# Softmax normalised before the transpose, and the attention output laid out by transfers, in a two-layer image kernel

## The chip, the cores and the metric

The kernel runs on one core of a Trainium2 chip. The metric is the time of one execution on the device in microseconds (us); lower is better. The time before is the median of three runs.

## The reference, cut to what matters

The input is 8 images of 384 channels, 64 x 64 pixels, in float32. Two layers follow, each a residual over a group norm.

Layer 0 is windowed attention. A layer norm over the channels, then queries, keys and values for 8 heads of 48 channels. Heads 0 to 3 ("branch 0") work in windows of 8 x 8 pixels, heads 4 to 7 ("branch 1") in the same windows on an image rolled by 4 pixels both ways, with a mask. Then a projection.

Layer 1 mixes channels, multiplies 8 x 8 patches in the frequency domain by a filter, applies a 3 x 3 convolution to each channel alone ("taps"), gates one half with the GELU of the other, and projects back.

```python
attn = jnp.einsum('bhnd,bhmd->bhnm', q, k) + bias (+ mask)
attn = jax.nn.softmax(attn, axis=-1)
out = jnp.einsum('bhnm,bhmd->bhnd', attn, v)
...
x = x + layer0(group_norm(x))      # out @ proj_w + proj_b
x = x + layer1(group_norm(x))      # w_in, patch filter, 3x3 taps, gelu gate, w_out
```

## The kernel before, in words

**Tiling.** An image is cut into 8 strips of 8 rows (512 pixels). A strip is a tile of 128 partitions by 3 x 512 values: channels on partitions, three groups. Each strip has 8 windows of 64 pixels. A *unit* is one branch of one strip; there are 8 x 8 x 2 = 128 of them.

**Attention of a unit.** `qk_tile` makes queries and keys (`pq`, three PSUM tiles; ScalarE moves them out, L420). `v_tile` makes the values with pixels on partitions (`pvv`, L454), and puts a column of ones beside each head's 48 channels, so that the product with the weights also gives their sum. `scores` makes the scores (`pS`): 32 matmuls of 64 x 64, four of them in the four quadrants of the array at a time. `weights`, on VectorE, adds the position bias (L482), takes each row's maximum (L486) and subtracts it (L489). `exponent` is one ScalarE instruction over 128 x 1024 (L495). `turn` transposes the exponentials on TensorE, 8 transposes `pT` (L72), and ScalarE copies them to `eT` (L505). `apply` multiplies them with the values: 32 matmuls of 64 x 49, `pA`, pixels on partitions. `normalise`, on VectorE, divides by the sums (L529, L530) into `o`. `put` turns `o` to channels on partitions, again by 8 TensorE transposes (`po`), and ScalarE and VectorE copy these into the strips' tiles `oT` (L553, L554, L561 to L563). Branch 1 goes to two strips, since its image is rolled. `project` multiplies `oT` by the projection (`pr`) and VectorE adds it to the input (`x_add`, L572).

**Layer norm.** The sums over channels are matmuls (`ln`); ScalarE copies them (L362), VectorE and ScalarE make the reciprocal deviation `lr` (L364 to L367). It is spread over all partitions by two transfers from SyncE's queue (SP): `lr` to a line in memory (L374), and the line to every partition as `rs` (L376). VectorE multiplies the strip by it: `y<-rs` (L389). Before that, the normalised input `y` comes from VectorE (L338) and its square `sq` from ScalarE (L347).

**Layer 1.** `mix` (`pt`), `transform` (`pf`, L627), `back` (`pz`) and `border` (ScalarE copies of `z`, L655 to L659); the taps on VectorE (L693 for the first on ScalarE, then L699, eight in turn for each of three channel groups); `gate`; `finish` (`pw`, with a PSUM tile of its own `pw2`, then L738 and L740). In the last image, some taps are matmuls with diagonal matrices (`conv_taps`, `pc`): five of group 1 in every strip, and in the last strip nine of group 1 and three of group 2.

**What orders the work.** Every piece of work is entered in a plan with a place, `at(place, piece, ...)`, and the plan is sorted. A unit takes one step of place, a strip two. Layer 1 of an image runs beside layer 0 of the next: strip by strip the two are interleaved. Matmuls keep the plan's order. The other engines' orders are made by the scheduler of the tile framework, with a few fixed dependences. Tiles come from pools with a set number of buffers, handed out in turn: whoever takes a buffer waits until the last reader of its former content is done. In PSUM there are four buffers "gemm" of one bank and two buffers "att" of two banks; `pS`, `pT`, `pA`, `po`, `pw2` and `pc` share the two. A common strip takes the "att" buffers in the order pA, pS, pw2, po, pT, pA, pS, po, pT.

**Empty instructions.** TensorE's instructions are counted as they are built (`FETCHES`, `WAITS`, `RUN_AT`), and empty ones are put among the long matmuls[...].

Of the kernel before, what the change touches and what calls it, by code (L numbers as in the profile page):

```python
# [27 lines left out]
C_SWAP = C_PICK + 2  # L28
N_CONST = C_SWAP + 128
WAITS = 5.325, -22  # L30
FETCHES = {"qk_tile": 12, "v_tile": 24, "project": 12, "scores": 128, "apply": 128, "turn": 16, "put": 16,
# [7 lines left out]
def block_kernel(ctx: ExitStack, tc: tile.TileContext, out, x, consts, fsel, wqk, wv, bqk, bv,  # L39
# [52 lines left out]
    swap = cst[:, C_SWAP:C_SWAP + P]  # L92
# [259 lines left out]
    def ln_sums(b, s):  # L352


        p = psum(f"ln_{b}_{s}")
        for to, t, n in ((0, ys[b, s], KC), (P, ys.pop((b, s, "sq")), 1 if summed(b, s) else KC)):
            for k in range(n):
                for j in range(4):
                    matmul(p[32 * j:32 * (j + 1), to:to + P], ones_c[:, 0:32], t[:, k, j * P:(j + 1) * P],
                           start=(k == 0), stop=(k == n - 1))  # L360
        m = sb.tile([P, 2 * P], F32, tag="lc", bufs=1, name=f"m_{b}_{s}")
        nc.scalar.copy(m, p[:, 0:2 * P])  # L362
        rc = sb.tile([P, P], F32, tag="lr", bufs=2, name=f"lr_{b}_{s}")
        nc.vector.tensor_tensor(rc, m[:, 0:P], m[:, 0:P], ALU.mult)  # L364
        nc.vector.tensor_tensor(rc, m[:, P:2 * P], rc, ALU.subtract)
        nc.scalar.activation(rc, rc, AF.Sqrt, bias=eps_t)
        nc.vector.reciprocal(rc, rc)  # L367
        if (b, s) == (0, 0):
            ys[b, s, "rc"] = rc
            return  # L370

        line = dr.tile([4, P], F32, tag="line", bufs=4, name=f"line_{b}_{s}")
        queue = nc.scalar if b == 0 and s < 2 else nc.sync
        queue.dma_start(out=line, in_=rc[0:P:32, :])  # L374
        rs = ys[b, s, "rs"] = row512("rs", 2, f"rs_{b}_{s}")
        queue.dma_start(out=rs, in_=bass.AP(line.tensor, line.offset, [[0, P], [1, ST]]))  # L376
# [63 lines left out]
    def v_tile(b, s, br, g):  # L440

        y = y2s[b, s] if br else ys[b, s]
        if g == 0:
            v = sb.tile([P, 4, 4, HD + 1], F32, tag="v", bufs=2, name=f"v_{b}_{s}_{br}")
            nc.gpsimd.memset(v[:, :, :, HD:HD + 1], 1.0)
            vs[b, s, br] = v
        v = vs[b, s, br]
        pvv = psum(f"pvv_{b}_{s}_{br}_{g}")
        for i in range(2):
            pair = 2 * g + i  # L450
            for k in range(KC):
                matmul(pvv[:, i * 192:(i + 1) * 192], y[:, k, pair * P:(pair + 1) * P],
                                 wv_sb[:, k, br * 192:(br + 1) * 192], start=(k == 0), stop=(k == KC - 1))
        nc.scalar.copy(v[:, 2 * g:2 * g + 2, :, 0:HD],  # L454
                       pvv[:, 0:384].rearrange("p (g h d) -> p g h d", g=2, h=4))
# [37 lines left out]
    def exponent(b, s, br):  # L493
        e = qks[b, s, br, "e"]
        nc.scalar.activation(e, e, AF.Exp)  # L495

# [11 lines left out]
    def apply(b, s, br):  # L508

        eT, v = qks.pop((b, s, br, "eT")), vs.pop((b, s, br))  # L510
        pA = psum2(f"pA_{b}_{s}_{br}")
        for i in range(2):
            for h in range(4):
                to = (i * 4 + h) * (HD + 1)
                for odd in range(2):
                    pair = 2 * i + odd
                    for q in range(2):
                        rows, half = slice(q * 64, (q + 1) * 64), (q + odd) % 2
                        col = pair * P + (h + q) % 2 * 64
                        matmul(pA[half * 64:(half + 1) * 64, odd, to:to + HD + 1],  # L520
                               eT[rows, h // 2, col:col + 64], v[rows, pair, h, :], start=True, stop=True)
        qks[b, s, br, "A"] = pA

    def normalise(b, s, br):
        nm = f"{b}_{s}_{br}"
        o = os_[b, s, br] = sb.tile([P, 2, 2, 192], F32, tag="o", bufs=1, name=f"o_{nm}")
        pA = qks.pop((b, s, br, "A"))[:, :, 0:8 * (HD + 1)].rearrange("p g (h d) -> p g h d", h=8)
        rc = small.tile([P, 2, 8], F32, tag="rc", bufs=2, name=f"rc_{nm}")
        nc.vector.reciprocal(rc.unsqueeze(3), pA[:, :, :, HD:HD + 1])  # L529
        nc.vector.tensor_tensor(  # L530
            o.rearrange("p g i (h d) -> p g (i h) d", d=HD),
            pA[:, :, :, 0:HD], rc.unsqueeze(3).to_broadcast([P, 2, 8, HD]), ALU.mult)
# [7 lines left out]
    def put(b, s, br):  # L540


        o = os_.pop((b, s, br))
        p = psum2(f"po_{b}_{s}_{br}")
        po = []
        for a in range(2):
            for pair in range(4):
                transpose(p[:, a, pair * P:(pair + 1) * P], o[:, pair % 2, pair // 2, a * 64:a * 64 + P],
                          swap if pair % 2 else ident)
            po.append(p[:, a].rearrange("p (w r c) -> p r w c", w=NS, r=WS))  # L550
        if br == 0:
            oT = out_tile(b, s)
            nc.scalar.copy(oT[:, 0].rearrange("p r (w c) -> p r w c", c=WS), po[0])  # L553
            nc.vector.tensor_copy(oT[64:P, 1].rearrange("p r (w c) -> p r w c", c=WS), po[1][64:P])  # L554
            return
        for half, oT in ((0, out_tile(b, s)), (1, out_tile(b, (s + 1) % NS))):
            to, of = slice(4 - 4 * half, 8 - 4 * half), slice(4 * half, 4 * half + 4)
            for rows, kt, src, copy in ((slice(0, 64), 1, po[0], nc.vector.tensor_copy),
                                        (slice(0, P), 2, po[1], nc.scalar.copy)):
                d = oT[rows, kt, to]  # L560
                copy(d[:, :, 4:60].rearrange("p r (w c) -> p r w c", c=WS), src[rows, of, 0:7])  # L561
                copy(d[:, :, 60:64], src[rows, of, 7, 0:4])
                copy(d[:, :, 0:4], src[rows, of, 7, 4:8])  # L563
# [101 lines left out]
    on_pe = {s: {1: 5} for s in range(NS)}  # L665
    on_pe[NS - 1] = {1: 9, 2: 3}

    def tap_matrices():
        d = strip("y", 3, "taps").rearrange("p k (t c) -> p (k t) c", c=P)
        for m, n, to in ((1, 9, 0), (2, 3, 9)):  # L670
            for i in range(n):
                nc.scalar.activation(d[:, to + i], ident, AF.Copy, scale=dw_sb[:, m, TAPS[i]:TAPS[i] + 1])
        zs["taps"] = {1: d[:, 0:9], 2: d[:, 9:12]}

    def conv_taps(b, s):
        pc = psum2(f"pc_{b}_{s}")
        for i, (m, n) in enumerate(on_pe[s].items()):
# [6 lines left out]
    def conv(b, s, m, tap):  # L684

        z = zs[b, s, m]
        n = on_pe[s].get(m, 0) if b == B - 1 else 0
# [59 lines left out]
    for b in range(B):  # L747
# [22 lines left out]
        for s in range(NS):  # L770
# [16 lines left out]
            for br in range(2):  # L787
# [10 lines left out]
                at(w + 1.07, normalise, b, s, br)  # L798
                at(w + 1.23, put, b, s, br)
# [12 lines left out]
        at(first + 1.90, second_std, b)  # L812
        if b == B - 1:
            at(first + 2, tap_matrices)
        for s in range(NS):
# [16 lines left out]
            if b == B - 1:  # L832
# [11 lines left out]
    for i, (piece, args) in enumerate(order):  # L844
        count += 4 * sum(on_pe[args[1]].values()) if piece is conv_taps else FETCHES.get(piece.__name__, 0)
# [19 lines left out]
def _constants():  # L865
# [6 lines left out]
    c[:, C_SWAP:C_SWAP + P] = np.roll(np.eye(P), 64, axis=1)  # L872
# [96 lines left out]
```

## Time and profile before

| what | value |
|---|---|
| time, median of 3 runs (lowest to highest) | 3695.2 us (3693.99 to 3695.85) |
| time of the profiled execution | 3693.57 us |
| its span, first to last instruction | 3691.7 us |
| mean clock granted to TensorE | 0.994 |
| transposes `po` (L72), 1024 | 133.0 us of records, overlapped |
| normalising, L529 and L530, 128 each | 29.8 and 122.5 us on VectorE |
| exp, L495, 128 | 135.3 us on ScalarE |
| share of the 16 transfer engines taken by SP's queue q1 | 28.4% |

The span is the time that the profile covers; 1.9 us of the profiled execution lie around it. The profile gives for each engine how long it was busy, and for each group of instructions the mean duration of one and the idle time of its engine just before, with the engine that ended it. Matmuls overlap, so their records add up to more than the time that passes; how long a run of matmuls takes is read from the start of one run to the start of the next in the timeline. "DVE" is VectorE, "ACT" ScalarE, "PE" TensorE, "POOL" GpSimd and "SP" SyncE.

### The profile page before, as it was taken

Reading aid. Unit: us, or ns where it says so; the run is one execution under the profiler, and the core shown is the slowest. Engines: PE = TensorE matmul, PEld = TensorE weight load, DVE = VectorE, ACT = ScalarE, POOL = GpSimd, SP = SyncE. Lnnn points to the kernel's source line nnn. Section 1 sums busy time; section 2 is a strip of 40 time slices with the busy share of each in tenths; the row PEclk is TensorE's granted clock in tenths of the full one; section 3 lists DMA queues with packets and bytes.
Section 4 is the critical chain, followed back from the end, with each engine's and each line's share of the span. In section 5 each row is a group of like instructions: output and inputs, shape, how many; then the busy total and the mean of one; then the engine's idle time right before and its main releaser. Section 6 shows DMA issues by size and latency. Waiting matters only on the chain.

```text
span 3691.7 us, 92911 instructions
## 1 busy us (share of the span) xinstructions
PE 3610.3 (98%) x38584; PEld 2342.0 (63%) x38584; DVE 2841.1 (77%) x4607; ACT 2384.6 (65%) x3946; POOL 426.9 (12%) x764
## 2 busy tenths in 40 slices
PE   6999999999999999999999999999999999999898
PEld 4666666666666666666666666666666666666554
DVE  5655578778878788877888778878788777777898
ACT  3776577667667576666766666666676666776442
POOL 4111111101111111111111111111111111110000
PEclk8999999999999999999999999999999999999999
DMA  4222223223323233223333223323233222222422
GB/s 121 87 101 82 77 93 126 84 90 127 118 92 108 79 120 132 96 83 117 118 107 107 104 90 118 119 81 118 98 110 119 92 90 93 93 81 84 152 103 78
DMA packets 144355, 377.07 MB, mean 102 GB/s; under 512 B 12288, under 2 KB 12876, under 8 KB 143948
## 3 DMA queue, kind: packets, MB, share of 16 engines
q1 hardware_dynamic: 139952, 370.60, 28.4%
q8 instruction: 319, 5.23, 0.6%
q0 software_dynamic: 2048, 0.15, 0.1%
q14 instruction: 88, 0.72, 0.1%
q10 hardware_dynamic: 1948, 0.37, 0.1%
HBM read 270.28 MB, written 100.79 MB: 101 GB/s over the span
## 4 chain that ended last, share of the span: by engine, by line
PE 87%; DVE 6%; DMA 3%; ACT 2%; issue 1%; SPq 0%; ACTq 0%; DVEq 0%
PE pq L62 25%; PE pr L62 13%; PE pvv L62 12%; PE pt L62 12%; PE pw L62 6%; DVE zz L699 3%; PE pS L62 3%; PE pA L62 3%; PE po L72 3%; PE pT L72 3%; PE pz L62 3%; PE pf L62 2%; PE ln L62 2%; DMA x_norm<-in_x_dram 1%; DMA x1d<-x_add 0%
## 5 line engine op out<-in xcount | busy, mean ns | idle before, releaser
L699 DVE SCALAR_TENSOR_TENSOR zz<-z,dw_sb,zz 128x512 f32<-128x512 f32 x1490 | 1082.0, 751 | 23.7 <-ACT z L658 11.2
L62 PE MATMUL pq<-y,wqk_sb 128*128 128x512 f32 x2160 | 990.1, 596 | 0.0
L62 PEld LDWEIGHTS pq<-y,wqk_sb 128*128 128x128 f32 x2160 | 402.3, 190 | 436.6 <-issue 403.7
L62 PE MATMUL pt<-wi_sb,xn 128*128 128x384 f32 x1536 | 534.6, 486 | 0.0
L62 PE MATMUL pr<-oT,wp_sb 128*128 128x512 f32 x1152 | 523.1, 592 | 0.5 <-DVE oT L563 0.5
L62 PE MATMUL pvv<-wv_sb,y 128*128 128x192 f32 x2880 | 495.8, 326 | 0.0
L62 PEld LDWEIGHTS pvv<-wv_sb,y 128*128 128x128 f32 x2880 | 471.7, 190 | 36.2 <-issue 23.2
L420 ACT ACTIVATE qab<-pq,bq_sb,cst 96x512 f32<-96x512 f32 (+1 forms) x256 | 198.0, 773 | 383.4 <-PE pq L62 381.5
L62 PEld LDWEIGHTS pt<-wi_sb,xn 128*128 128x128 f32 x1536 | 286.1, 190 | 200.9 <-issue 38.5
L420 ACT ACTIVATE kcd<-pq,vec 32x512 f32<-32x512 f32 x512 | 348.8, 681 | 9.1
L62 PEld LDWEIGHTS pr<-oT,wp_sb 128*128 128x128 f32 x1152 | 211.1, 190 | 223.9 <-issue 213.5
L402 POOL COPY y<-y 128x384 f32<-128x384 f32 x112 | 100.2, 895 | 1528.5 <-PE pvv L62 1021.3
L610 ACT COPY t<-pt 128x384 f32<-128x384 f32 x256 | 124.2, 485 | 176.9 <-PE pt L62 172.9
L364 DVE TENSOR_TENSOR lr<-m 128x128 f32<-128x128 f32 x64 | 18.7, 292 | 281.0 <-ACT m L362 281.0
L693 ACT ACTIVATE zz<-z,dw_sb 128x512 f32<-128x512 f32 x183 | 133.9, 733 | 156.2 <-PE pw L62 141.8
L350 POOL TENSOR_TENSOR sq<-sq 128x512 f32<-128x512 f32 x122 | 156.6, 1284 | 628.1 <-ACT sq L347 623.3
L420 ACT ACTIVATE qcd<-pq,bq_sb,cst 96x512 f32<-96x512 f32 (+1 forms) x256 | 197.4, 771 | 44.7 <-PE pq L62 41.2
L454 ACT COPY v<-pvv 128x384 f32<-128x384 f32 x256 | 121.0, 478 | 156.7 <-PE pvv L62 156.5
L572 DVE SCALAR_TENSOR_TENSOR x_add<-pr,vec,x_add 128x512 f32<-128x512 f32 x192 | 143.5, 747 | 93.6 <-PE pr L62 91.7
L62 PE MATMUL pw<-zz,wo_sb 128*128 128x512 f32 (+1 forms) x512 | 182.3, 499 | 0.0
L420 ACT ACTIVATE kab<-pq,vec 96x512 f32<-96x512 f32 (+1 forms) x256 | 174.3, 681 | 8.3 <-PE pq L62 6.5
L72 PEld LDWEIGHTS pT<-cst,e 128*128 128x128 f32 x1024 | 119.0, 141 | 66.6 <-issue 39.6
(142 smaller groups left out, 5294.9 us busy)
## 6 DMA issues: line engine op xcount, KB each, us to landing
x_add<-in_x_dram SPq DMA_DIRECT2D x64, 768.0 KB, 9.8
x1d<-x_add SPq DMA_DIRECT2D x64, 768.0 KB, 3.7
x_mix<-x1d SPq DMA_DIRECT2D x64, 768.0 KB, 4.4
x_finish<-x1d SPq DMA_DIRECT2D x64, 768.0 KB, 6.0
out_dram<-x_finish SPq DMA_DIRECT2D x64, 768.0 KB, 3.8
x_norm<-in_x_dram SPq DMA_DIRECT2D x61, 768.0 KB, 7.5
x_stats<-in_x_dram SPq DMA_DIRECT2D x56, 768.0 KB, 7.9
rs<-line SPq DMA_DIRECT2D x62, 256.0 KB, 3.0
```

The lines of the kernel that those rows point to most:

```text
L62: tc.keep_in_program_order(nc.tensor.matmul(*args, **kw))
L72: tc.keep_in_program_order(nc.tensor.transpose(*args, **kw))
L350: nc.gpsimd.tensor_tensor(sq[:, 0, :], sq[:, 0, :], sq[:, k, :], ALU.add)
L364: nc.vector.tensor_tensor(rc, m[:, 0:P], m[:, 0:P], ALU.mult)
L402: nc.gpsimd.tensor_copy(dst[:, :, :, :, 0:4], src[:, :, :, :, 4:8])
L420: return nc.scalar.activation(dst[to:to + n], pq[of:of + n], AF.Identity, bias=bias[of:of + n], scale=scale)
L454: nc.scalar.copy(v[:, 2 * g:2 * g + 2, :, 0:HD], pvv[:, 0:384].rearrange("p (g h d) -> p g h d", g=2, h=4))
L572: nc.vector.scalar_tensor_tensor(t[:, m, :], pr, bp_sb[:, m:m + 1], t[:, m, :], ALU.add, ALU.add)
L610: nc.scalar.copy(t1, pt[:, 0:C])
L693: nc.scalar.activation(zz.rearrange("p (r c) -> p r c", c=SW), z[:, 1:9, 1:SW + 1], AF.Copy, scale=dw_sb[:, m, 4:5])
L699: i = nc.vector.scalar_tensor_tensor(acc.rearrange("p (r c) -> p r c", c=SW), z[:, dy:dy + 8, dx:dx + SW], dw_sb[:, m, TAPS[tap]:TAPS[tap] ...
```

## The change

The row sums are no longer made with the values. After exp, VectorE sums each row of 64, takes the reciprocal and multiplies the row by it; the transposed weights are then already normalised. The column of ones and `normalise` go. (`v` keeps 16 zero columns behind its 768, which the last head's 64-column block reaches into.)

`apply` swaps its operands: the values stand in the array, 64 columns of them for a head of 48 channels, and the weights stream through. So `pA` has channels on partitions, and `put` needs no transposes. ScalarE copies `pA` to `o`, pixels in image order (two copies for branch 0, four for branch 1), and transfers on SP's queue bring `o` to the partitions of `oT`: 5 for branch 0, twice 5 for branch 1, of 16 to 48 partitions each.

The tile `o` is larger, and `lr` has one buffer for two. The matrix `swap` goes. `put` stands at `w + 1.07`, where `normalise` was. The last strip of image 6 gets five taps of group 1 as matmuls, the last strip of image 7 five of group 2 for three; the matrices take two tiles. The second group norm's deviation of the last image is entered at 1.995 instead of 1.90. The constants of the empty instructions are set anew.

```diff
-WAITS = 5.325, -22
-FETCHES = {..., "put": 16, ...}
+WAITS = 6.63, -32
+FETCHES = {...}
...
-        rc = sb.tile([P, P], F32, tag="lr", bufs=2, name=f"lr_{b}_{s}")
+        rc = sb.tile([P, P], F32, tag="lr", bufs=1, name=f"lr_{b}_{s}")
...
-            v = sb.tile([P, 4, 4, HD + 1], F32, tag="v", bufs=2, name=f"v_{b}_{s}_{br}")
-            nc.gpsimd.memset(v[:, :, :, HD:HD + 1], 1.0)
+            v = sb.tile([P, 16 * HD + 16], F32, tag="v", bufs=2, name=f"v_{b}_{s}_{br}")
+            nc.gpsimd.memset(v[:, 16 * HD:], 0.0)
...
     def exponent(b, s, br):
         e = qks[b, s, br, "e"]
         nc.scalar.activation(e, e, AF.Exp)
+        rc = small.tile([P, 2 * NS], F32, tag="rc", bufs=2, name=f"rc_{b}_{s}_{br}")
+        nc.vector.tensor_reduce(rc, e, AX.X, ALU.add)
+        nc.vector.reciprocal(rc, rc)
+        nc.vector.tensor_tensor(e, e, rc.unsqueeze(2).to_broadcast([P, 2 * NS, 64]), ALU.mult)
...
     def apply(b, s, br):
         eT, v = qks.pop((b, s, br, "eT")), vs.pop((b, s, br))
         pA = psum2(f"pA_{b}_{s}_{br}")
-        for i in range(2):
-            for h in range(4):
-                to = (i * 4 + h) * (HD + 1)
...
-                        matmul(pA[half * 64:(half + 1) * 64, odd, to:to + HD + 1],
-                               eT[rows, h // 2, col:col + 64], v[rows, pair, h, :], start=True, stop=True)
+        for hp in range(2):
+            for pair in range(4):
+                to = (hp * 4 + pair) * 64
+                for par, q in ((0, 0), (1, 1), (0, 1), (1, 0)):
+                    rows, of = slice(q * 64, (q + 1) * 64), (pair * 4 + hp * 2 + par) * HD
+                    col = pair * P + (par + q) % 2 * 64
+                    matmul(pA[par * 64:(par + 1) * 64, q, to:to + 64], v[rows, of:of + 64],
+                           eT[rows, hp, col:col + 64], start=True, stop=True)
...
-    def normalise(b, s, br):
...
     def put(b, s, br):
-        o = os_.pop((b, s, br))
-        p = psum2(f"po_{b}_{s}_{br}")
-        po = []
-        for a in range(2):
-            for pair in range(4):
-                transpose(p[:, a, pair * P:(pair + 1) * P], o[:, pair % 2, pair // 2, a * 64:a * 64 + P],
-                          swap if pair % 2 else ident)
...
+        pA = qks.pop((b, s, br, "A")).rearrange("p o (h w r c) -> p o h w r c", h=2, w=4, r=WS)
+        o = sb.tile([P, 2, ST], F32, tag="o", bufs=1, name=f"o_{b}_{s}_{br}")
+
+        def columns(first, n, step=16, c=WS):
+
+            return bass.AP(o.tensor, o.offset + first, [list(o.ap[0]), [ST, 2], [step, n], [SW, WS], [1, c]])
+
         if br == 0:
...
+            for q in range(2):
+                nc.scalar.copy(columns(q * WS, 4), pA[:, q])
+            parts = ((slice(0, WS), 0, out_tile(b, s)),)
+        else:
+            nc.scalar.copy(columns(4, 4), pA[:, 0])
+            nc.scalar.copy(columns(12, 3), pA[:, 1, :, 0:3])
+            nc.scalar.copy(columns(60, 1, c=4), pA[:, 1, :, 3:4, :, 0:4])
+            nc.scalar.copy(columns(0, 1, c=4), pA[:, 1, :, 3:4, :, 4:8])
+            parts = ((slice(4, 8), 0, out_tile(b, s)), (slice(0, 4), 256, out_tile(b, (s + 1) % NS)))
+        edge = (P, 64)[br]
+        for rows, of, oT in parts:
+            n = (rows.stop - rows.start) * SW
+            for h in range(4):
+                row = h % 2 * 64 - h * HD
+                for a, z in ((h * HD, min((h + 1) * HD, edge)), (max(h * HD, edge), (h + 1) * HD)):
+                    if a < z:
+                        to = a + br * P + (64 if a >= edge else 0)
+                        nc.sync.dma_start(out=oT[to % P:to % P + z - a, to // P, rows],
+                                          in_=o[row + a:row + z, h // 2, of:of + n])
...
-    on_pe = {s: {1: 5} for s in range(NS)}
-    on_pe[NS - 1] = {1: 9, 2: 3}
+    on_pe = {(B - 1, s): {1: 5} for s in range(NS - 1)}
+    on_pe[B - 2, NS - 1] = {1: 5}
+    on_pe[B - 1, NS - 1] = {2: 5, 1: 9}
...
-                at(w + 1.07, normalise, b, s, br)
-                at(w + 1.23, put, b, s, br)
+                at(w + 1.07, put, b, s, br)
...
-        at(first + 1.90, second_std, b)
+        at(first + (1.90 if b < B - 1 else 1.995), second_std, b)
```

## The prediction

> **What bounds the kernel now.** I read the page first, busy shares and then the chain that ended last, and after these the timelines of single strips of images 4 and 6.
>
> ```profile
> PE 3610.3 (98%) x38584; PEld 2342.0 (63%) x38584; DVE 2841.1 (77%) x4607; ACT 2384.6 (65%) x3946; POOL 426.9 (12%) x764
> PE 87%; DVE 6%; DMA 3%; ACT 2%; issue 1%; SPq 0%; ACTq 0%; DVEq 0%
> ```
>
> TensorE is busy all the time and 87% of the chain is its matmuls. In the steady state it does not stop at all: the stretches from 1852.8 to 1907.5 and from 1907.5 to 1962.2 us, one strip each, show 54.70 us of PE in 54.70 us. So each microsecond that TensorE need not work is won, and each that it must wait is lost.
>
> What decides is how near the softmax comes to the transposes `pT` that need it. Times below count from the end of a unit's `pS` (its last score). Strip 4 of image 4, branch 1, has `pS` end at 1937.1:
>
> ```profile
> 1935.93 0.95 DVE L367 RECIPROCAL lr<-lr 128x128 f32<-128x128 f32 x1 [0.17 <-ACT lr L366]
> 1937.03 0.96 DVE L530 TENSOR_TENSOR o<-pA,rc 128x768 f32<-128x768 f32 x1
> 1938.83 0.68 DVE L482 TENSOR_TENSOR e<-pS,bias 128x512 f32<-128x512 f32 x1
> 1940.20 1.22 DVE L486 TENSOR_REDUCE mx<-e 128x16 f32<-128x1024 f32 x1
> 1941.60 1.76 DVE L389 TENSOR_TENSOR y<-y,rs 128x1536 f32<-128x1536 f32 x1 [0.18 <-DMA rs<-line]
> 1943.28 1.22 DVE L489 TENSOR_TENSOR e<-e,mx 128x1024 f32<-128x1024 f32 x1
> ```
>
> ```profile
> 1945.87 1.06 ACT L495 ACTIVATE e<-e 128x1024 f32<-128x1024 f32 x1
> ```
>
> ```profile
> 1950.85 1.04 PE L72 MATMUL pT<-cst,e 128*128 128x128 f32 x8
> ```
>
> exp ends at +9.8 and `pT` starts at +13.8, so 3.9 us are free. `y<-rs` (layer norm of a later strip) sits in the middle of the chain and starts when its transfer lands, at +4.5. In the first two strips of an image less TensorE work lies between, and nothing is free; this is strip 1 of image 6 (`pS` end 2665.2), where TensorE already waits 1.10 us for exp:
>
> ```profile
> 2668.71 5.32 PE L62 MATMUL pq<-y,wqk_sb 128*128 128x512 f32 x12
> 2675.13 1.09 PE L72 MATMUL pT<-cst,e 128*128 128x128 f32 x8 [1.10 <-ACT e L495]
> ```
>
> The third view is the one wait of TensorE on L530:
>
> ```profile
> 2636.34 0.66 PE L62 MATMUL pw<-g,wo_sb 64*64 64x256 f32 x8 [0.87 <-DVE o L530]
> ```
>
> `pw2` of `finish` takes the PSUM buffer that `pA` held (two buffers "att", taken in turn: pA, pS, pw2). Once L530 was late, and TensorE stood. Normally L530 ends at +0.4, and `pw2` is due at about +0.8 (the first eight `pw` records take 0.7 us from +0.0).
>
> [...]VectorE idles 0.18 us at `y<-rs` with the softmax's next step queued behind. [...]The trace has 3.0 us for `rs<-line` (256 KB) from issue to landing.
>
> **The change, part by part.** Durations are from the page's groups and these timelines; back to back an instruction costs about 0.1 us less than its mean. Orders are those of the instruction lists of the two built kernels.
>
> *Removed on TensorE:* the 8 transposes `po` of a unit. From 1914.02 to 1914.89 they take 0.88 us; 128 units give 112.6 us at most, kept only where TensorE sets the pace.
>
> *Widened:* `pA` goes from 49 to 64 columns, again 32 matmuls. `pS`, with 64, takes 0.95 us against 0.88: 128 x 0.05 = 6 us.
>
> *VectorE:* L529, L530 and the copies L554, L561-L563 go (29.8 + 122.5 + 44.5 + 48.4 + 40.1 = 285 us). Row sums, reciprocal and product over 128x1024 come. They are priced as L486 (1.22), L529 (0.27) and L489 (1.24): 2.7 us x 128 = 349 us. VectorE is not full (45.7 of 54.7 us), so the 64 us more are free as busy time. But these three stand between exp and `pT`, and the built order puts other work among them. Branch 1 of a common strip reads: three adds, `y<-rs`, maximum, subtract, tap, residual, tap, statistics, SUM, tap, reciprocal, tap, PRODUCT. `y<-rs` stands ahead of the maximum now. The walk: the adds start at +0.7 (L530 is gone) and end at +2.0; `y<-rs` waits for its transfer, +4.5, or +4.9 with two of the new transfers ahead of it on SP's queue[...] (bounds +4.5 and +6.2); it ends at 6.5, maximum 7.7, subtract 8.9, exp 10.0. VectorE meanwhile does tap 0.66, residual 0.67, tap 0.66, statistics 0.61 to 11.5, SUM 12.7, tap, reciprocal, tap 14.3, PRODUCT 15.55. `pT` starts at +15.6; TensorE was ready at 13.8 - 0.88 = 12.9, and `pr`, `pvv` and `pz` stand behind it. Against before, `pT` comes 1.8 us later, the saved `po` already counted. By kind of branch-1 unit:
> - 34 common ones: 34 x 1.8 = 61 us.
> - Strip 5 of images 1 to 6, where `y<-rs` comes even ahead of the adds: +16.5 for +13.8, 6 x 2.7 = 16.
> - Strip 0 of images 2 to 7 (four taps and three tiny steps in the gap): +16.1 for +8.9, 6 x 7.2 = 43.
> - Strip 1 of images 2 to 7 (four taps): +15.6 for +9.7, 6 x 5.9 = 35.
> - Image 0, strips 0 and 1 of image 1 and the last two units, walked alike: +9.
>
> Sum 164 us. Branch 0 of images 1 to 7 has 8.3 us free and needs 5.5 to 6 more; there `po` is won: 56 x 0.88 = -49.
>
> *Release of `pA`, an added wait:* now ScalarE frees it, by two or four copies into `o` (0.5, 0.4, 0.1, 0.1 = 1.1 us back to back). Queued ahead on ScalarE are the second `v` copy (ready at -3.8 before the next `pS` end), the square of `y` (1.48), then nine copies and scalings of `z` (6.45 to 9.53 in 1906.45 to 1909.53: 3.1 us). From -3.3 that gives -1.8, +1.3, and with `o` +2.4. `pw2` was due at +0.8, so TensorE waits 1.55 us, and all of `pw`, `pq` behind it. Where statistics of the next image precede the last `y` on VectorE (strips 2 and 3, 11 times), the square is late by 1.2 more: 2.75. Finishes in the dense part: 52; 41 x 1.55 + 11 x 2.75 = 94 us. Bounds: 0, if ScalarE comes early, and 140.
>
> *Transfers:* 5 + 10 per strip, 960 in all, on SP. Issues there last 0.3 to 0.6 us for like ones, so ten need 3 to 6 us of a queue that mostly waits (L741 alone 1112 us). `pr` reads `oT` about a unit later (20 us): nothing. For the last image's end, `oT` comes by transfer: about +4 with the taps. *Taps:* five more on TensorE for strip 7 of image 6 (5 x 0.86), two more at the end, against four and two VectorE steps of 0.66 us in a stretch where VectorE is as full as TensorE (223 and 225 of 251 us): put at nothing, bounds -4 and +6. *Layout:* one buffer for `lr` waits only for a transfer done a strip ago: nothing.
>
> Sum: 164 - 49 + 94 + 6 + 4 = +219. The profiled execution took 3693.6 us (span 3691.7); with it 3912.6. The median of the runs is 1.6 above it: **3914 us**.
>
> **Rivals.**
> - *ScalarE frees `pA` in time* (its queue runs ahead while TensorE waits at `pT`): 3914 - 94 = 3820. Against it: the square cannot start before `v` and the last `y`.
> - *SP delays `rs`*: two issues ahead of it of 1.2 us, as `x_stats` shows at 1916.83, make `rs` 1.3 us later in 52 units: 3914 + 68 = 3982. For it: SP waits for `o` between `line` and `rs`; against it: the `line` transfer takes that time anyway.
> - *The other side, faster:* the three steps fit into the free 3.9 us. They are 2.7 us long, L529 and L530 (1.16 us) go ahead of the chain, and the table load (1.28) no longer waits for the subtract. If `pT` of branch 1 is ready at +12.9, all of `po` is won: 3695.2 - 112.6 + 6 + 4 = 3593. Against it: `rs` lands at +4.5 whatever VectorE does, and strips 0 and 1 have nothing free at all.
> - That `po` might not be gone is excluded: the built list has none.
>
> **Numbers.** Chances: main case 0.65 (its own range 3840 to 3985, from the bounds of `rs` and half the `pw2` wait), free `pA` 0.14, late `rs` 0.12, faster 0.07, and 0.02 that losses and gains cancel within 0.2% (what a measurement can tell from no change). The range goes from 3780, under the first rival, to 4000; it leaves out the faster case and the ends. Faster by over 0.2% 0.07, within 0.2% 0.02, slower 0.91.
>
> **What would show it.** Right: `pT` with waits on VectorE's product of 2.5 to 3 us in common branch-1 units and 6 to 8 in strips 0 and 1, summing to some 220 us (they count from the shortened work, and so are larger than the delays above); `pw` with waits of 1 to 3 us on ScalarE's copies of `o`; a common strip of 57 to 58.5 us for 54.7; PE near 90% (3510 of 3912 us). Wrong: `pT` of branch 1 at +13 or earlier, `y<-rs` with idle time far from 2.5 to 3 us, or new waits of `pr` for `oT`.

## The result, and the profile after

The changed kernel takes 4025.0 us (median of 4 runs, 4024.0 to 4026.4) against 3694.6 us for the kernel before on the same chip: ratio 1.0895, 95% interval 1.0882 to 1.0908, 330 us slower. The forecast was 3914 us, 219 us slower, with a range up to 4000. The direction and the places were right; the size was 111 us short, and the range with it. The profiled execution took 4024.0 us (span 4022.2).

Busy shares, and the shares of the chain that ended last (the first two lines that the prediction showed of before):

```profile
PE 3626.3 (90%) x37574; PEld 2296.5 (57%) x37574; DVE 2874.6 (71%) x4281; ACT 2438.7 (61%) x3883; POOL 359.5 (9%) x764
PE 52%; DVE 25%; ACT 9%; DMA 8%; issue 3%; SPq 3%; ACTq 0%; DVEq 0%
```

TensorE has 1010 matmul records fewer (the 1024 transposes `pT` leave 1024 records, the 4096 matmuls `pA` 8192) and is busy 16 us longer. Its share of the chain falls from 87% to 52%; VectorE, ScalarE and the transfers now set the pace between its stretches. The costliest groups name both waits (busy us, mean ns of one, then idle time before it and who ended it):

```profile
L71 PE MATMUL pT<-cst,e 128*128 128x128 f32 x1024 | 170.1, 321 | 272.3 <-DVE e L497 263.1
L387 DVE TENSOR_TENSOR y<-y,rs 128x1536 f32<-128x1536 f32 x63 | 110.8, 1758 | 231.4 <-DMA rs<-line 231.4
```

TensorE's waits by line (total us, times, longest) give the second place:

```profile
PE pT L71 <- DVE e L497: 263.1, 65, 9.0
PE pw L61 <- ACT o L549: 70.1, 51, 3.4
```

Before, the same two stood at 8.9 and 5.0 us:

```profile
PE pT L72 <- ACT e L495: 8.9, 9, 1.5
PE pw L62 <- DVE o L530: 5.0, 6, 1.2
```

So the transposes wait 263 us for the product, the last of the three new steps, and `pw` 70 us for ScalarE's copies of `o`. The groups' rows hold a third thing that no list of waits shows: matmuls that became longer. These are the rows of `pr`, before and then after:

```profile
L62 PE MATMUL pr<-oT,wp_sb 128*128 128x512 f32 x1152 | 523.1, 592 | 0.5 <-DVE oT L563 0.5
```

```profile
L61 PE MATMUL pr<-oT,wp_sb 128*128 128x512 f32 x1152 | 561.8, 629 | 0.0
```

The same 1152 records take 39 us more, those of `pT` 36 us (133.6 to 170.1) and those of `pvv` 20 us (495.8 to 515.9).

**One unit.** Image 4, strip 3, branch 1 has its `pS` end at 2052.8. First VectorE:

```profile
2053.28 0.68 DVE L480 TENSOR_TENSOR e<-pS,bias 128x512 f32<-128x512 f32 x1
...
2058.99 1.76 DVE L387 TENSOR_TENSOR y<-y,rs 128x1536 f32<-128x1536 f32 x1 [4.37 <-DMA rs<-line]
2060.67 1.21 DVE L484 TENSOR_REDUCE mx<-e 128x16 f32<-128x1024 f32 x1
2061.91 1.22 DVE L487 TENSOR_TENSOR e<-e,mx 128x1024 f32<-128x1024 f32 x1
...
2065.64 1.20 DVE L495 TENSOR_REDUCE rc<-e 128x16 f32<-128x1024 f32 x1
...
2067.42 0.25 DVE L496 RECIPROCAL rc<-rc 128x16 f32<-128x16 f32 x1
...
2068.21 1.22 DVE L497 TENSOR_TENSOR e<-e,rc 128x1024 f32<-128x1024 f32 x1
```

VectorE stands 4.37 us at `y<-rs`, with the maximum and the subtract behind it: the last of the three adds, which the maximum reads, ends at 2054.62, and the maximum starts at 2060.67. SyncE's queue shows when `rs` was issued (here, then in the unit of before that the prediction showed, `pS` end 1937.1):

```profile
2052.52 0.59 SPq L372 DMA_DIRECT2D line<-lr  x1
2053.20 1.68 SPq L559 DMA_DIRECT2D oT<-o  x2
2054.97 0.54 SPq L374 DMA_DIRECT2D rs<-line  x1
```

```profile
1936.91 0.55 SPq L374 DMA_DIRECT2D line<-lr  x1
1938.58 0.33 SPq L376 DMA_DIRECT2D rs<-line  x1
```

Two transfers of values take 1.68 us ahead of `rs<-line`, which is issued at +2.2 instead of +1.5. The larger part of the lateness comes after the issue: `y<-rs` starts 4.0 us after it, and 3.0 us after it before (1938.58 to 1941.60). Then TensorE:

```profile
2063.17 2.74 PE L61 MATMUL pq<-y,wqk_sb 128*128 128x512 f32 x6
2069.48 1.97 PE L71 MATMUL pT<-cst,e 128*128 128x128 f32 x8 [3.58 <-DVE e L497]
2071.24 4.76 PE L61 MATMUL pr<-oT,wp_sb 128*128 128x512 f32 x6
2075.84 1.46 PE L61 MATMUL pvv<-wv_sb,y 128*128 128x192 f32 x8
```

The six records of `pr` behind `pT` read the same `oT` as the six at 2060.59, and start only at 2071.24, after the wait. From start to start `pT` takes 1.76 us (0.87 before, 1950.85 to 1951.72) and six records of `pr` take 4.60 us (2.58 for six of them ahead of the wait, 2060.59 to 2063.17). The stretches of this window say why (length, busy time of PE, PEld, DVE, ACT, POOL, then TensorE's clock, transfer share and GB/s):

```profile
2065.80:2069.40 3.60, 0.10 (x1) 0.00 (x0) 3.60 (x6) 3.55 (x6) 0.00 (x0) 0.87 0.46 177
2069.40:2075.00 5.60, 5.52 (x13) 3.46 (x14) 5.60 (x11) 3.11 (x4) 0.00 (x0) 0.50 0.01 3
2068.50:2075.30 6.80, 5.82 (x13) 3.46 (x14) 6.80 (x11) 4.00 (x6) 0.00 (x0) 0.50 0.01 2
2075.40:2085.00 9.60, 9.24 (x258) 7.88 (x256) 4.88 (x9) 5.52 (x14) 2.60 (x3) 1.00 0.01 2
```

The clock falls to half at 2068.5, 2.6 us into the wait, and is back at 2075.3, 5.8 us after the matmuls have started again. The prediction had left the clock out.

The clock records of the whole trace show 56 stretches at 0.50: 25 of 3.4 us, 23 of 6.8, seven of 10.2 and one of 17.1, 331 us in all, with TensorE busy in 232 of them. Before, there were seven stretches, 48 us with 31 busy. Matmuls took about twice as long in them (1.76 us for 0.87, 4.60 for 2.58), so half of the busy time is an estimate of what they cost: 116 us, and 15 before, 101 us more. Which waits lead to one can be counted too (the first 150 and the last 200 us left out): all 26 waits of 3.5 us or more did, 15 of the 24 from 3.0 to 3.5 us, 8 of the 15 from 2.0 to 3.0, and 1 of the 22 from 1.2 to 2.0.

**Where the 330 us lie.** I split 126 of the 128 units at `pS` end and `pT` start and took the differences between the two traces:

| part | predicted | measured |
|---|---|---|
| branch 1, `pS` to `pT` | +164 | +203 |
| of it strips 0 and 1, images 2 to 7 | +78 | +88 |
| branch 0, `pS` to `pT` (`po` won, `pw` waiting) | -49 + 94 = +45 | +46 |
| both branches, `pT` to the next `pS` (`pA`, and the slow clock) | +6 | +80 |
| end | +4 | about 0 |

Branch 1 is 39 us worse, and behind `pT` there are 74 us more than foretold; the estimate above puts 92 us of half clock there, and the waits there are 9 us shorter than before. Branch 0 came out at the number worked out, but partly by luck: TensorE's idle time there rose by 73 us, where waits of 94 were foretold, and the half clock behind the longer waits of `pw` added an estimated 16.

A sum over the whole span agrees. TensorE's idle time is 396 us (4022.2 - 3626.3), and the prediction's 3510 us busy of 3912 meant 402. So the waits were right in sum: those of `pT` are longer than foretold (272 us for some 220), those of `pw` shorter (70 for 94), and some 30 us of waits of the kernel before are gone. The busy time is 3626 us for 3510, 116 us too long, and that is about the whole shortfall of 111 us: matmuls at half clock.

### The profile page after: what moved, and what is told of

It reads as the page before. It is cut to its first block, busy times and chain, and to the rows that moved or that the text cites. A ratio compares the mean times of both kernels' runs of the same rounds, so it can differ in the third digit from the quotient of the medians.

```text
span 4022.2 us, 93913 instructions
## 1 busy us (share of the span) xinstructions
PE 3626.3 (90%) x37574; PEld 2296.5 (57%) x37574; DVE 2874.6 (71%) x4281; ACT 2438.7 (61%) x3883; POOL 359.5 (9%) x764
## 4 chain that ended last, share of the span: by engine, by line
PE 52%; DVE 25%; ACT 9%; DMA 8%; issue 3%; SPq 3%; ACTq 0%; DVEq 0%
PE pq L61 12%; PE pt L61 10%; PE pvv L61 9%; DVE zz L698 9%; PE pr L61 7%; PE pw L61 5%; DMA rs<-line 5%; PE pT L71 3%; DVE y L387 2%; ACT z L652 2%; SPq L559 2%; DVE st L245 2%; DVE e L497 2%; DVE rc L495 2%; DMA x_stats<-in_x_dram 2%
## 5 line engine op out<-in xcount | busy, mean ns | idle before, releaser
L61 PE MATMUL pr<-oT,wp_sb 128*128 128x512 f32 x1152 | 561.8, 629 | 0.0
L61 PE MATMUL pvv<-wv_sb,y 128*128 128x192 f32 x2880 | 515.9, 335 | 0.0
L61 PEld LDWEIGHTS pvv<-wv_sb,y 128*128 128x128 f32 x2880 | 493.5, 197 | 38.4 <-issue 22.8
L71 PE MATMUL pT<-cst,e 128*128 128x128 f32 x1024 | 170.1, 321 | 272.3 <-DVE e L497 263.1
L61 PEld LDWEIGHTS pr<-oT,wp_sb 128*128 128x128 f32 x1152 | 231.8, 206 | 267.8 <-issue 252.3
L71 PEld LDWEIGHTS pT<-cst,e 128*128 128x128 f32 x1024 | 141.9, 166 | 346.4 <-DVE e L497 172.0
L480 DVE TENSOR_TENSOR e<-pS,bias 128x512 f32<-128x512 f32 (+2 forms) x200 | 108.3, 548 | 256.8 <-PE pS L61 256.8
L387 DVE TENSOR_TENSOR y<-y,rs 128x1536 f32<-128x1536 f32 x63 | 110.8, 1758 | 231.4 <-DMA rs<-line 231.4
L493 ACT ACTIVATE e<-e 128x1024 f32<-128x1024 f32 x128 | 135.3, 1057 | 183.1 <-DVE e L487 181.4
L400 POOL COPY y<-y 128x384 f32<-128x384 f32 x112 | 58.3, 521 | 1692.7 <-PE pvv L61 1103.2
```

The costliest lines, as they stand in the source:

```text
L61: tc.keep_in_program_order(nc.tensor.matmul(*args, **kw))
L71: tc.keep_in_program_order(nc.tensor.transpose(*args, **kw))
L387: nc.vector.tensor_tensor(y, y, rs.unsqueeze(1).to_broadcast([P, KC, ST]), ALU.mult)
L480: nc.vector.tensor_tensor(e5[:, odd, :, a:z, :], pS[:, odd, :, a:z, :], bias_t[br, kind, odd].unsqueeze(2).to_broadcast([P, 2, z - a, 64]) ...
```

## The experiments

My theory after the comparison: three delays of TensorE (the product late because `rs` is later still than assumed; `pw` held by ScalarE; and the slow clock after waits). The rival for each is named in its expectation. All ratios are to the kernel before, run on the same chip; "split as above" means the parts of the table.

**1. The three steps taken out.**

```diff
-        rc = small.tile([P, 2 * NS], F32, tag="rc", bufs=2, name=f"rc_{b}_{s}_{br}")
-        nc.vector.tensor_reduce(rc, e, AX.X, ALU.add)
-        nc.vector.reciprocal(rc, rc)
-        nc.vector.tensor_tensor(e, e, rc.unsqueeze(2).to_broadcast([P, 2 * NS, 64]), ALU.mult)
```

> The changed kernel with the three VectorE steps between exp and the transposes left out (row sums, reciprocal, product; its weights are not normalised). Theory (these steps, behind the late rs, make TensorE wait at pT, and each long wait halves its clock for a while): pT is ready at +11 after the scores' end, before TensorE is at it (+12.9) except in strips 0 and 1, where some 3 us stay; of the 330 us lost some 300 come back, about 3720 us, and the pT->pS stretches of branch 1 go back from 12.8-13.3 to about 11.4 us. Rival (the 960 transfers on SP's queue cost the time): they are all still there, so over 3900 us. Rival (the release of pA by ScalarE): also still there, over 3850 us.

The weights of this kernel are not normalised. Measured 3794.8 us, 1.0267 (1.0252 to 1.0283): 230 of the 330 us go, less than expected. The scheduler reordered VectorE, and `pz` now waits 39.5 us (34 times) for `x_add`, which comes later; `pw` still waits 56 us. So the three steps, where they stand, carry most of the loss, and taking them out uncovers the next wait.

**2. ScalarE's copies of `o` given to VectorE.**

```diff
-                nc.scalar.copy(columns(q * WS, 4), pA[:, q])
+                nc.vector.tensor_copy(columns(q * WS, 4), pA[:, q])
```

The four of branch 1 are changed alike.

> The changed kernel with the copies of pA to o on VectorE, which had made the release before, in place of ScalarE. Theory: the waits of pw for the copies of o (51 of them, 70 us on matmuls and up to 116 us seen at the weight loads, the longest 3.4 to 4.3) go, and with them slow clock behind the longest; the maximum stands ahead of y<-rs again; 3880 to 3930 us. Rival (this wait only takes time that the chain would lose anyway at the next pT): within 20 us of 4025 us.

Measured 3902.9 us, 1.0564 (1.0548 to 1.0580), 122 us less than the change. The wait of `pw` is gone from the list, that of `pT` is 237 us. The release of `pA` by ScalarE is a real cost, more than its 70 us of listed waits; this edit also put the maximum ahead of `y<-rs` again, so not all of the 122 us belong to the release. Split as above, 82 us go ahead of `pT` in branch 0, where the release is, and 36 ahead of `pT` in branch 1.

**3. The transfers of `o` issued by GpSimd.**

```diff
-                        nc.sync.dma_start(out=oT[to % P:to % P + z - a, to // P, rows],
+                        nc.gpsimd.dma_start(out=oT[to % P:to % P + z - a, to // P, rows],
```

> The changed kernel with the transfers oT<-o issued by GpSimd instead of SyncE. Theory: rs is issued at +1.5 again instead of +1.8 to +2.4 and lands about 0.7 us earlier, in some 55 units on the chain: 20 to 60 us less, 3965 to 4005 us, unless GpSimd's own work (the shifted strips, the squares) comes too late for it. Rival (the transfers as such, their traffic, are the cost): no gain, 4025 us or more.

Measured 3985.2 us, 1.0794 (1.0774 to 1.0814): 40 us less. In branch 1 the subtract ends 0.7 to 1.0 us earlier and `pT` starts as much earlier; `pw` waits 71 us as before. Split as above, branch 1 ahead of `pT` falls by 37 us, to about the 164 predicted, so the 39 us by which that term was short come from the values on SyncE's queue. The total of 40 agrees by chance: 14 us go behind `pT` as well, and 18 come back in branch 0, with more half clock behind `pw`.

**4. Useless matmuls in the gap.** 204 matmuls of 0.86 us were put ahead of `pT` in branch 1 of images 2 to 7: eight in strips 0 and 1 (12 units), three in the others (36 units).

```diff
         pT = psum2(f"pT_{nm}")
+        for _ in range(fillers(b, s, br)):
+            matmul(pT[:, 0], ident, wqk_sb[:, 0, 0:4].rearrange("p j c -> p (j c)"), start=True, stop=True)
```

> The changed kernel with useless matmuls (identity by 512 columns of a weight tile, 0.86 us each) ahead of pT in branch 1 of images 2 to 7: three in strips 2 to 7, eight in strips 0 and 1, so that TensorE works where it had waited; 156 matmuls, 134 us of added work. Theory (after a wait of 3 us or more the clock is halved for some 5 us): the waits shrink by what is added, the clock stays near 1.0, the pT->pS stretches go back to about 11.4 us, and the time falls by 50 to 75 us, to 3950 to 3975 us. Rival (those stretches are longer for another reason, traffic or late operands): no gain, 4025 us or up to 30 us more.

The expectation's 156 matmuls and 134 us are a miscount, six units of strips 0 and 1 for twelve; the trace has 408 records, two for each matmul. Measured 3966.9 us, 1.0736 (1.0718 to 1.0754): 175 us of added work make the kernel 58 us *faster*. The rows show how:

```profile
L61 PE MATMUL pT<-wqk_sb,cst 128*128 128x512 f32 x408 | 182.9, 592 | 0.0
L61 PE MATMUL pr<-oT,wp_sb 128*128 128x512 f32 x1152 | 531.5, 600 | 1.2 <-DMA oT<-o 1.2
L71 PE MATMUL pT<-cst,e 128*128 128x128 f32 x1024 | 140.8, 282 | 99.1 <-DVE e L497 93.5 <-ACT kcd L418 5.6
```

`pr` is back from 629 to 600 ns and `pT` from 321 to 282. TensorE's idle time falls by 174 us (396 to 222), which is just the added work; the gain lies in shorter matmuls (30 us in `pr`, 29 in `pT`, 16 in `pvv`). The half clock's estimated cost falls from 116 to 50 us. The other engines' work is unchanged; only TensorE stood still less. This shows the slow clock as a cost of its own.

**5. The three steps alone, in the kernel before.** The output path stays as before; a plain copy takes the place of `normalise`.

```diff
         nc.scalar.activation(e, e, AF.Exp)
+        rc = small.tile([P, 2 * NS], F32, tag="rc", bufs=2, name=f"rc_{b}_{s}_{br}")
+        nc.vector.tensor_reduce(rc, e, AX.X, ALU.add)
...
-        nc.vector.reciprocal(rc.unsqueeze(3), pA[:, :, :, HD:HD + 1])
...
+        nc.vector.tensor_copy(o.rearrange("p g i (h d) -> p g (i h) d", d=HD), pA[:, :, :, 0:HD])
```

> The kernel before with one part of the change alone: the weights are divided by their sums after exp by the same three VectorE steps, and L529/L530 become a plain copy of pA to o on VectorE; transposes po, the copies to oT and SP's queue stay as before. Theory (the three steps make pT late, most where little TensorE work lies ahead of it): subtract ends at +7.4 as before, the built order is tap, copy, residual, tap, SUM, tap, reciprocal, tap, PRODUCT, so pT at about +14.2: 0.4 us late in common branch-1 units, some 5 us in strips 0 and 1, with slow clock behind these; 3780 to 3840 us. Rival (the transfers and ScalarE's release are the cost, not the softmax): within 20 us of 3694 us.

Measured 3858.7 us, 1.0441 (1.0425 to 1.0456): +163, a little over the range. Split as above, +106 lie ahead of `pT` and +51 behind it; of the 51, an estimated 31 are half clock, and 11 are short waits for which the trace names no releaser. So half of the loss comes without any of the new transfers or ScalarE copies. The longer matmuls are there too: `pT` has a mean of 294 ns for 273, `pvv` 334 for 326.

**6. `y<-rs` put behind the subtract.**

```diff
-        nc.vector.tensor_tensor(y, y, rs.unsqueeze(1).to_broadcast([P, KC, ST]), ALU.mult)
+        i = nc.vector.tensor_tensor(y, y, rs.unsqueeze(1).to_broadcast([P, KC, ST]), ALU.mult)
+        if "soft" in zs:
+            behind(i, zs["soft"], mybir.DependencyClass.NoSync, "softmax first")
```

> The changed kernel with y<-rs held behind the subtract on VectorE (an order without a semaphore), so that maximum, subtract and exp no longer stand behind the transfer of rs. Theory: subtract at +4.5 in place of +9.7, pT at about +13 in common branch-1 units, against +12.9 of TensorE; in strips 0 and 1 some 5 us of wait stay; 3770 to 3830 us. Rival (rs only fills time that the chain has anyway): over 3950 us.

Measured 3843.2 us, 1.0398 (1.0383 to 1.0414): 182 us less from one dependence.

```profile
PE pw L61 <- ACT o L551: 103.0, 51, 2.9
PE pT L71 <- DVE e L499: 65.1, 25, 5.8
```

In common strips the subtract of branch 1 ends at +4.5 instead of +10.0 (medians of 27 units), and `pT`'s wait for the product falls from 263 to 65 us. Split as above, 189 us go ahead of `pT` in branch 1 and 60 behind it, and 70 come back in branch 0. What comes back is at `pw` (waits of 103 us for 70, and half clock behind them), which is why it came out above the expected range. Most of the loss ahead of `pT` came not from the length of the three steps but from their place behind a transfer.

**7. `turn` later in the plan.**

```diff
-                at(w + 0.64, turn, b, s, br)
+                at(w + 0.865, turn, b, s, br)
```

> The changed kernel with the transposes pT entered at w + 0.865 in place of w + 0.64, so that in branch 1 a projection and the values (6.5 us, 3.9 us in strips 0 and 1) come ahead of them; VectorE's work is unchanged. Theory: no wait at pT in common units (TensorE ready at +19), some 5 us in strips 0 and 1; clock near 0.98; the waits of pw stay, so 3770 to 3840 us. Rival (the time is bound by VectorE or transfers, TensorE's place in the order is indifferent): over 3980 us.

Measured 3953.7 us, 1.0696 (1.0678 to 1.0714): only 71 us less, a clear miss. The wait had moved:

```profile
PE pA L61 <- ACT eT L507: 106.2, 37, 3.7
PE pT L71 <- DVE e L497: 59.0, 17, 5.6
```

`pA` stands close behind `pT` now, and ScalarE's copy of the transposed weights (1.0 us, behind what is queued on ScalarE) lies between. I had counted only the distance from scores to `turn`, not that from `turn` to `apply`.

**8. Edits 2, 6 and 7 together.**

> The changed kernel with VectorE copies of pA, y<-rs behind the subtract and the later pT together. Theory: all new waits are gone but 1 to 2 us in strips 0 and 1, and what the removed transposes saved remains: 3590 to 3650 us, faster than before. Rival (the loss is not in these three waits): over 3700 us.

Measured 3721.9 us, 1.0067 (1.0041 to 1.0093), 303 of the 330 us. Expected was a clear gain over the kernel before; by its time alone the run lies on the rival's side (over 3700, the loss is not in these three waits). `pA` waits 71 us for `eT` (43 times), which the later `turn` brought in, so four more runs vary the places.

**9 to 12. Where `turn` and `apply` stand.** All four keep edits 2 and 6. Number 9 leaves `turn` at w + 0.64; 10 has it at w + 0.77, and so has 11, with edit 3 besides:

```diff
-                at(w + 0.64, turn, b, s, br)
+                at(w + 0.77, turn, b, s, br)
```

Number 12 moves three pieces:

```diff
-                at(w + 0.64, turn, b, s, br)
-                at(w + 1.00, apply, b, s, br)
-                at(w + 1.07, put, b, s, br)
+                at(w + 0.865, turn, b, s, br)
+                at(w + 1.06, apply, b, s, br)
+                at(w + 1.09, put, b, s, br)
```

> The version with all three edits, but the turn back at its place of the changed kernel (w + 0.64). Theory, that in the version with all three TensorE lost its time because the moved turn stands so close to the weighted values that these wait for ScalarE's copy of the transposed weights (71 us, 43 waits there): that wait goes to 0, and what comes back is the wait for the third step in strips 0 and 1 of branch 1, 40 to 70 us with its slow clock: 3700 to 3745 us. Rival, that VectorE's 160 us of added copies and sums set the time: nothing but the turn has changed and VectorE's work is the same, so within 10 us of 3722.

> All three edits, the turn at w + 0.77, between the two places tried. Theory (the turn has to be 3 us of TensorE work clear of the weighted values, and 13 us behind the scores): both waits are mostly gone, 3675 to 3710 us, at or below the kernel before. Rival, that VectorE's added work sets the time: within 10 us of 3722.

> The same with the transfers of the values issued by GpSimd instead of SyncE. With y behind the subtract, nothing on SyncE that TensorE waits for is late any more: within 8 us of the run with the turn at w + 0.77 if the SyncE queue cost only through rs; 10 to 30 us less if the loads and the first spread map behind the transfers still cost something.

> All three edits with the turn at w + 0.865, and the weighted values moved from w + 1.00 to w + 1.06, behind the next unit's scores, the copies from w + 1.07 to w + 1.09. Theory (distance of the turn and the values is what is late): the 71 us of waits for ScalarE's copy go, since about 4 us of scores lie between: 3665 to 3700 us unless the later copies make the finish of the strip wait. Rival (VectorE's work): within 10 us of 3722.

| run | us | ratio (interval) | `pT` waits | `pA` waits |
|---|---|---|---|---|
| 9, `turn` at 0.64 | 3728.7 | 1.0093 (1.0078 to 1.0108) | 98.7 | none listed |
| 10, `turn` at 0.77 | 3698.5 | 1.0012 (1.0005 to 1.0019) | 74.4 | none listed |
| 11, the same, transfers on GpSimd | 3691.5 | 0.9992 (0.9984 to 1.0001) | 76.2 | 2.1 |
| 12, `apply` behind the scores | 3722.0 | 1.0075 (1.0060 to 1.0090) | 31.2 | 30.9 |

Runs 9 and 10 do with the waits what the theory said, though `pT` waits longer in 9 than expected (98.7 us for 40 to 70). The time of 9 fits both the theory and the rival (VectorE's added work is the bound); 10 goes below 3712, which the rival excluded. Number 11 is 7 us below 10: with `y<-rs` out of the way, SyncE's queue costs almost nothing. Number 12 is a miss, at just the time that its rival gave: the waits of `pA` shrink by half against run 8 (71 to 31 us), but `pT` waits more (31 us for 12) and new waits of `pw` appear (21.8 us for `z`, 9.2 for `e`). Number 11 equals the kernel before, so about 100 us of removed work were still lost. Its trace has two places. In branch 1 of strips 0 and 1 `pT` still waits 4.4 to 4.8 us, and in a common strip `pw` is late (strip 4 of image 4, `pS` end at 1911.4):

```profile
1911.18 1.02 PE L61 MATMUL pw<-g,wo_sb 64*64 64x512 f32 x2
1912.73 1.51 PE L61 MATMUL pw<-g,wo_sb 64*64 64x512 f32 x14 [0.53 <-ACT z L657]
1914.18 1.12 PE L61 MATMUL pw<-zz,wo_sb 128*128 128x512 f32 x2
```

The sixteen records ahead of `zz` take 3.0 us from start to start; before, they took 1.44.

**13 and 14. These two places.** 13 is 11 with a later `turn` where little TensorE work lies between:

```diff
-                at(w + 0.77, turn, b, s, br)
+                at(w + (0.865 if br and s < 2 else 0.77), turn, b, s, br)
```

14 is 13 with an order on ScalarE, where `zs["z"]` is the latest copy of `z` from `pz`:

```diff
-        nc.scalar.activation(sq, ys[b, s], AF.Square)
+        i = nc.scalar.activation(sq, ys[b, s], AF.Square)
+        if "z" in zs:
+            behind(i, zs["z"], mybir.DependencyClass.NoSync, "z first")
```

> As the run with the turn at w + 0.77 and GpSimd's transfers, but in branch 1 of strips 0 and 1 the turn at w + 0.865, where less TensorE work lies between. In the run with all three edits these units took 18.1 us from scores to scores, against 23.4 with w + 0.77: 12 units x 5.3 us = 64 us less, about 3628 us (3615 to 3650), below the kernel before. Rival, that VectorE's added work is the bound (83% busy): what is won there comes back as later waits, 3675 to 3695 us.

> The same, with ScalarE's square of y put behind its copies of z. If pw, once a strip, waits for z because the square (1.48 us) stands ahead of it and itself waits for VectorE's y: some 1.5 us in about 40 strips, 40 to 60 us less than the run before it, 3565 to 3610 us. Rival, that z is late on its own (the matmuls that make it): no change, within 8 us of it.

Number 13: 3636.0 us, 0.9840 (0.9826 to 0.9853), as expected, 56 us less than 11. Split as above, the 12 units of strips 0 and 1 in images 2 to 7 give 65 us, for 64 expected, and branch 0 gives 23 back. Number 14: 3619.0 us, 0.9797 (0.9784 to 0.9810), only 17 us less than 13 where 40 to 60 were expected. In the strip just shown `pw` takes 1.52 us again, but common strips gained some 0.5 us of branch 0 on average and not 1.5, and in strips 1 and 2 `pw` still waits for VectorE's copies of `o`:

```profile
PE pw L61 <- DVE o L553: 21.7, 12, 2.4
PE pT L71 <- DVE e L501: 14.8, 15, 3.4
```

So the change, re-timed, is 75 us faster than the kernel before, of the 112.6 - 6 = 106 us that TensorE works less. Of the 31 us that are missing, 18 are idle time of TensorE (99 us, 81 before; the two waits above and one of 10.8 us at `pA` are the largest new ones), and an estimated 6 are half clock (21 us, 15 before). The rest stays open.

## Why the prediction was wrong in size

**The order on VectorE, right.** The prediction read from the built order that `y<-rs` now stands ahead of the maximum and said what follows: maximum, subtract, exp and three steps all behind a transfer. Experiment 6 takes 182 us away by that order alone.

**"`y<-rs` waits for its transfer, +4.5, or +4.9": the first failed step.** The walk took `rs` at +4.9, near the bottom of its own bounds (+4.5 to +6.2). In 27 common units (strips 2, 3, 4 and 6 of images 1 to 7) `y<-rs` starts at +5.9 in the median (5.4 to 6.6). The issue came as the walk assumed, 0.4 us later than before (+1.86 for +1.46). What failed is the time from there: 3.8 us from issue to the start of `y<-rs`, where it had been 3.0 and the walk kept 3.0. With the values issued by GpSimd (experiment 3) the issue is back at +1.46, and 3.6 us remain; why the transfer takes longer beside the new ones was not isolated. From there the lengths held: subtract ends at +10.0 for 8.9, exp at +11.1 for 10.0, the product at +16.3 for 15.55, and `pT` starts at +16.4 for 15.6. So `pT` is 0.8 us later than foretold in common units, 26 us in 34 of them; strips 0 and 1 add 10 (88 for 78). Term: 164 predicted, 203 measured; experiment 3 takes 37 us off it. The rival "SP delays `rs`" had the place right and its size at 68; it looked for the delay in the issues, and most of it was in the transfer. It was no alternative but a part.

**"`pA` ... 6 us": the missing term.** Nothing but the wider `pA` was put down behind `pT`, and 74 us more than that arose there; this is the larger failed step. Each wait was priced at its own length. The wait of 3.58 us in the unit above cost more: `pT` lost 0.89 us and `pr` 2.02 us by the half clock. Experiment 4, with 175 us of added work and 58 us less time, shows that it is the standing still that costs; experiment 5 has an estimated 31 us of half clock behind `pT` with only the three steps added. The waits that the prediction itself foretold, 2.5 to 3 us and 6 to 8 us, were long enough to ask for this: of those measured from 2.0 to 3.0 us 8 of 15 led to half clock, and of those of 3.5 us or more all 26.

**"`pw2` waits for ScalarE's release", right in kind, its number by luck.** 94 us with 49 us won gave +45; measured +46. The waits are 70 us and not 94, 1.37 us in the mean (70.1 / 51) for 1.55 and 2.75 predicted, and the half clock behind the longer ones makes up most of the difference. What was not foreseen is the long one of strip 1, 3.40 us, where ScalarE also loads a table (1.28 us) and makes three `xn` (2.28 us) ahead of the copies.

**The sum.** 219 + 39 (branch 1) + 74 (behind `pT`, the clock) + 1 (branch 0) - 4 (end) = 329, for 330 measured. The retuned empty instructions, the moved taps and the single buffer of `lr` were not tried alone. The signs foretold were a common strip of 57 to 58.5 us (59.4 in strip 4 of image 4), `pT` waiting 2.5 to 3 and 6 to 8 (mostly 2.5 to 4.5, and 8 to 9 in strips 0 and 1), PE at 90% (90%, but with 16 us more of busy time where 100 less was expected). Two slips of the prediction changed little: TensorE waits for L530 six times before, 5.0 us in all, not once; and 0.95 against 0.88 us for the wider `pA` is 0.07 us, 9 us in all and not 6.

**The faster rival.** It needed `pT` of branch 1 ready at +12.9, and spoke of `rs` and of strips 0 and 1 as what stood against it. Both were obstacles in fact: with `rs` out of the chain and strips 0 and 1 given their own place the kernel is 2.0% faster. That took the copies on VectorE, the values on GpSimd and the square behind `z` as well (experiment 14), so it is not the change as it stands.

## What to carry to other kernels

When a step is added between two matmuls, walk the engine's built order and ask what stands at its head. Here `y<-rs`, waiting for its transfer, put off the subtract behind it to +10.0, where it ended at +4.5 with the order changed, and moving it was worth more than the steps themselves (182 us in experiment 6, when all three steps alone cost 163 in experiment 5). Price a long wait of TensorE at its length plus the half-clock stretch that follows (here all 26 waits of 3.5 us or more had one, and 8 of the 15 from 2.0 to 3.0 us), and look for it in the mean duration of the matmuls behind the wait, not in the list of waits. Moving a consumer later only helps if the next consumer keeps its own distance: count both gaps.

## What the runs showed of the hardware

- In a wait of 3.6 us TensorE's clock fell to 0.50 and stayed there for 6.8 us, 5.8 of them with matmuls. 56 such stretches of 3.4 us or a multiple of it cost an estimated 116 us in the changed kernel. 175 us of useless matmuls in the gaps made it 58 us faster.
- The transfers between partitions (16 to 48 partitions, five or ten at a time) took SyncE's queue 609 us for 960 issues, 0.63 us each, about as much as the issue of a load of 768 KB (0.62 to 0.66 us in the unit shown). The same 960 issued by GpSimd raised its busy time from 381 to 855 us, and the kernel was 7 us faster (runs 10 and 11).
- `rs<-line` (256 KB) took 3.0 us from issue to landing before, and 3.7 us with the values' transfers issued by GpSimd beside it (medians, experiment 3).
